# One group of silu(z) per chunk, a new layout of a chunk's pieces, and attention's first loads split over two queues

## The chip, the cores and the metric

The kernel runs on one core of one Trainium2 chip. Its time is the device time of one execution in microseconds. The kernel before takes 6737.77 us, the median of 3 runs (6736.29 to 6739.21). One execution was profiled.

## The reference, cut to what matters

Two layers with a residual each, on x of shape (4, 384, 64, 64) in fp32. Each layer first applies a group norm over 32 groups of channels. Layer 0 is a selective state-space layer over the 4096 positions of an image:

```python
xn = layernorm(tokens(gn(x))) * ln_w + ln_b
xb, z = split(xn @ in_proj_w.T)             # 768 channels each
xc = silu(causal_conv4(xb) + conv_b)
dt, Bm, Cm = split(xc @ x_proj_w.T)         # 24, 16, 16
dt = softplus(dt @ dt_w.T + dt_b)
h = exp(dt * A) * h + (dt * xc) * Bm        # a step per position; 768 channels x 16 states
y = sum_n(h * Cm) + xc * D
x = x + (y * silu(z)) @ out_proj_w.T
```

Layer 1 is an attention over a 7x7 neighbourhood with 12 heads, edge padding, a bias by relative place, softmax, a projection and a residual.

## The kernel before, in words

**Chunks and steps.** Layer 0 goes through 44 chunks: four images, each cut into pieces of 372 positions (the last has 376). A chunk holds 768 channels as six blocks `d` of 128 partitions. The 16 states come in four groups `g` of four. A step is one pair (d, g), so a chunk has 24 steps, and a step has four scans, one for each state: 96 scans in a chunk. A scan is one instruction of VectorE along the positions.

**What a step needs.** `carry` copies the state from the previous chunk into column 0 of a tile h (ScalarE). `drive` writes (dt*xc)*B into the tile, for one to four states at a time, on VectorE ("V", from the PSUM bank `dtxps`) or on GpSimd ("G", from a copy `dtx` in SBUF). `decay` computes exp(dt*A) for one state into one of three PSUM banks `das` (ScalarE). `scan` runs over it in place. `last_states` copies the last column away (ScalarE). `times_c` multiplies the tile by C (GpSimd). `sums` adds it up by transposing matmuls into the bank `yps` (TensorE). There are six h tiles (`HBUFS`). With three decay banks, ScalarE can be at most three scans ahead of VectorE: the decay for scan n needs scan n-3 to be done.

**The order.** All pieces of work are entered with a time, a tick, by `put`, sorted by tick and then emitted. A step is 16 ticks, a scan 4, a chunk (`CHUNK`) 384; a decay stands 5 ticks before its scan. The tables `AT` (the ticks of each kind of piece, relative to the first scan of the piece's chunk) and `DRIVES` (tick, step, engine, first state, number of states) fix the rest. A piece with a negative tick runs beside the chunk before. The class `Written` makes every engine keep the emitted order, SyncE's DMA queue too: an instruction that waits holds up all behind it on its engine. An engine that isn't held up may run ahead of its ticks.

**Tables of ScalarE.** Silu and softplus need table sets other than that of exp and ln, which is used everywhere else; each group (`silu`, `softplus`) ends with a load of the exp set. A chunk has two groups of silu(xc), two of silu(z) and two of softplus, each for three blocks: twelve loads. In the order, the two groups of silu(z) stand at ticks 4 and 75.

**Beside the scans** run, for the next chunk, group norm, layer norm, `in_proj` (12 products, each with a weight tile `w_in` loaded from DRAM through three buffers by `load_w`), the convolution and the small projections; for the chunk before, `gate`, `out_proj` and `residual`; and in later chunks a part of attention's keys, queries and values of images that are already done (the `key_` and `value_` pieces, with tiles xk, wk, yk, xv, vo).

**The passage to attention.** Attention goes over 32 stripes of 8 rows. A score of stripe 0 needs the keys `kt` of stripe 0 with three rows of stripe 1 copied into them by GpSimd (`surround`), the queries `q`, the bias by place, and output tiles in a pool `sb1`, whose memory is that of the state-space layer's main pool. Short-lived tiles (the set `short`) lie in a pool of their own, `prep`. `begin_attention` closes it once its last user has been emitted, and opens a pool `early` there, into which the first keys (stripes 0 and 1), the first queries, the first values `vw` and the bias are loaded through SyncE's queue. In the order before it stands at tick 597 of the last chunk, which is after that chunk's first residual. Whatever doesn't lie in `early` waits until the state-space layer's pool is free, that is until the last of its readers and writers, including the stores of the last rows of x1, has ended.

Of the kernel before, what the change touches and what calls it, by code (L numbers as in the profile page):

```python
# [8 lines left out]
F32 = mybir.dt.float32  # L9
# [5 lines left out]
P = 128  # L15
C = 384
NJ = C // P
# [5 lines left out]
NG = 4  # L23
# [7 lines left out]
TM = max(SIZES)  # L31
# [1 line left out]
STEPS = ND * NQ  # L33
STEP = 16
CHUNK = STEP * STEPS
SILU_X = SILU_Z = ((0, 1, 2), (3, 4, 5))
HBUFS = 6
CWBUFS = 3
KT = 256


AT = dict(
    load_x=(-732,),
    gn=(-656, -656, -704),
    ln_mean=(-634,),
    ln_centre=(-631,),
    ln_square=(-549, -548, -568),
    ln_var=(-540, -533, -531),
    ln_rstd=(-523,),
    ln_scale=(-520,),  # L50
    halo=(-582,),
    load_w=(-556, -419, -340, -366, -306, -365, -138, -149, -106, -103, -67, -32),
    in_proj=(-411, -388, -340, -343, -251, -321, -128, -134, -80, -33, -46, 23),
    in_bias=(-392, -387, -336, -319, -226, -286, -122, -121, -77, -30, -34, 36),
    conv=(-381, -317, -283, -227, -212, -214),
    conv_bias=(-366, -294, -257, -192, -201, -210),
    silu_x=(-253, -132),
    x_proj=(-123, -112),
    x_rows=(-100,),
    dt_mm=(-93, -56),  # L60
    softplus=(-90, -55),
    load_b=(-43, -46, -32, -29),
    load_c=(22, 15, 60, 71),
    silu_z=(4, 75),
    gate=(130, 241, 255, 327, 392, 462),
    out_proj=(462, 466, 569, 586, 588, 590),
    load_res=(371, 352, 527),
    residual=(502, 605, 617),
    out_stats=(681, 683, 692),
    dt_to_bank=(-43, 8, 91, 152, 218, 275),  # L70
    dt_times_x=(-32, 17, 91, 163, 226, 289),
    dtx_copy=(-21, 31, 101, 168, 230, 306),
    skipped=(-17, 37, 160, 180, 269, 336),
    turned_out=(97, 178, 241, 305, 363, 413),
    back=(107, 221, 250, 321, 381, 457),
    carry=(
        -4, -56, -29, 7, 36, 54, 24, 68, 102, 110, 116, 151, 176, 183, 160, 223, 247, 236,
        254, 289, 286, 297, 314, 334,
    ),
    last_states=(  # L80
        25, 33, 58, 67, 80, 100, 112, 135, 171, 168, 192, 197, 212, 236, 244, 255, 282, 289,
        309, 323, 343, 362, 384, 388,
    ),
    times_c=(
        37, 39, 72, 79, 95, 102, 115, 157, 173, 176, 203, 220, 237, 239, 257, 258, 292, 302,
        311, 339, 351, 369, 392, 394,
    ),
    sums=(
        53, 59, 76, 80, 109, 130, 149, 171, 181, 203, 224, 225, 246, 277, 278, 288, 308, 325,
        329, 353, 365, 384, 397, 412,  # L90
    ),
    x_stats=(-41, 24, 79, 381),
    x_norm=(12, 182, 194, 198, 211, 231, 247, 257, 271),
    out_norm=(319, 401, 414, 424, 442, 465, 482, 493, 507),
    value_load=(287, 147, 318),
    value_norm=(395, 214, 384),
    value_mm=(418, 238, 392),
    value_out=(424, 247, 410),
    value_store=(596, 251, 491),
    load_cv=(-473, -346, -314, -235, -259, -344),  # L100
    key_load=(44, 213),
    key_norm=(93, 69, 126, 276, 234, 288),
    key_mm=(135, 139, 181, 303, 305, 348),
    key_out=(143, 150, 191, 307, 315, 358),
    key_store=(289, 467),
)

DRIVES = (
    (-3, 0, "V", 0, 4), (0, 1, "G", 0, 3), (7, 1, "V", 3, 1), (7, 2, "V", 0, 4),
    (15, 3, "G", 0, 4), (39, 4, "G", 0, 1), (60, 5, "V", 3, 1), (61, 4, "G", 2, 2),  # L110
    (63, 4, "V", 1, 1), (67, 6, "V", 0, 4), (72, 5, "G", 0, 3), (74, 7, "V", 2, 1),
    (101, 7, "G", 0, 2), (105, 7, "G", 3, 1), (108, 8, "V", 0, 4), (126, 10, "G", 3, 1),
    (130, 9, "V", 0, 2), (132, 10, "V", 2, 1), (134, 9, "G", 2, 2), (135, 10, "G", 0, 2),
    (158, 11, "G", 0, 4), (183, 12, "V", 3, 1), (184, 12, "V", 0, 3), (184, 14, "V", 0, 4),
    (191, 13, "G", 0, 4), (228, 15, "G", 3, 1), (236, 15, "G", 0, 3), (241, 17, "V", 0, 1),
    (242, 17, "G", 1, 3), (251, 16, "V", 2, 1), (255, 16, "V", 0, 2), (255, 16, "V", 3, 1),
    (258, 18, "V", 0, 3), (264, 18, "G", 3, 1), (292, 20, "V", 0, 4), (293, 19, "G", 0, 4),
    (312, 21, "G", 0, 1), (330, 21, "V", 1, 3), (333, 22, "V", 0, 4), (344, 23, "G", 0, 4),
)
TX = 512  # L120
NXT = L // TX
# [6 lines left out]
HP = HW + 2 * PAD  # L128
# [5 lines left out]
RW, CW = RB + WS - 1, CB + WS - 1  # L134
NK = RW * CW
NCH = 2
# [32 lines left out]
def two_layers(  # L169
# [59 lines left out]
    def load(shape, src, name, pool=const):  # L229
        t = pool.tile(shape, F32, name=name)  # L230
        dq.dma_start(t, src)
        return t
# [106 lines left out]
    def load_stripe_keys(dq, kt, s):  # L339
        b, r = s // NXT, s % NXT  # L340
        for m in range(NJ):
            dq.dma_start(
                kt[:, m, PAD : PAD + RB, PAD : PAD + HW],
                kdr[b][m * P : (m + 1) * P, r * TX : (r + 1) * TX].rearrange(
                    "p (r c) -> p r c", r=RB
                ),
            )

    def load_stripe_queries(dq, q, s):
        b, r = s // NXT, s % NXT  # L350
        dq.dma_start(
            q, qdr[b][:, r * TX : (r + 1) * TX].rearrange("(k p) t -> p k t", p=P)
        )

    def load_pair_values(dq, vw, k):

        s, p = k // NPAIR, k % NPAIR
        b, r = s // NXT, s % NXT
        for e in range(2):
            for c in range(NCH):  # L360
                y, x0 = RB * r + c * RW // NCH, (2 * p + e) * CB
                dq.dma_start(vw[:KN, e, c, :], vdr[b][y : y + RW // NCH, x0 : x0 + CW, :])

    def state_space_layer(eng):
        te, ve, se, ge, _ = eng
# [4 lines left out]
        with ExitStack() as es:  # L370
# [15 lines left out]
            with tc.tile_pool(name="fold", bufs=1, side="right") as fold, tc.tile_pool(  # L386
                name="ps_fold", bufs=1, space=PSUM
            ) as fps:
                w_in = load([P, NJ, 2 * DI], in_wT.rearrange("(k p) m -> p k m", p=P), "w_in", fold)
# [70 lines left out]
            prep = preps.enter_context(  # L460
                tc.tile_pool(name="prep", bufs=1, reuse_waits="tile", side="right")
            )
            short = {"xn", "sq", "w_in", "xb", "cw", "xd", "xk", "yk", "wk", "xv", "vo"}

            free, kind_of = {}, {}

# [10 lines left out]

            def done(t):
                free[kind_of[id(t)]].append(t)

            def bank():
                return tile_of([P, 512], "mm", 3, ps_m)
# [370 lines left out]
            scans, drives, dtx, skip, turned = {}, {}, {}, {}, {}  # L853
# [280 lines left out]
            early = {}  # L1134

            def begin_attention():
                preps.close()
                home = ctx.enter_context(
                    tc.tile_pool(name="early", bufs=1, reuse_waits="tile", side="right")
                )  # L1140
                kt = early["kt"] = [
                    home.tile([P, NJ, RW, HP], F32, name=f"kt{s}") for s in range(2)
                ]
                q = home.tile([P, NJ, TX], F32, name="q0")
                vw = home.tile([P, 2, NCH, C], F32, name="vw0")
                bias = early["bias"] = home.tile([P, NH, NK], F32, name="bias")
                early["q"], early["vw"] = [q], [vw]
                for s in range(2):
                    load_stripe_keys(dq, kt[s], s)
                load_stripe_queries(dq, q, 0)  # L1150
                load_pair_values(dq, vw, 0)
                for e in range(2):
                    dq.dma_start(bias[e * QB : (e + 1) * QB].rearrange("p h k -> p (h k)"), bm)

            put(
                CHUNK * (len(chunks) - 1) + 1 + max(
                    max(AT[name]) for name in ("key_store", "value_store", "in_bias", "conv")
                ),
                begin_attention,
            )  # L1160
# [16 lines left out]
    def attention_layer(eng, gm1, qkb, pjb, early, mv):  # L1177
        te, ve, se, ge, dq = eng
        scale = HD**-0.5
        stripes = NB * NXT  # L1180
        with ExitStack() as es:
# [33 lines left out]
            def kt_of(s):  # L1215
                return ring([P, NJ, RW, HP], "kt", 4, s)

            def q_of(s):
                return ring([P, NJ, TX], "q", 3, s)
# [4 lines left out]
            def vw_of(k):  # L1224
                return ring([P, 2, NCH, C], "vw", 3, k)
# [39 lines left out]
                )  # L1265
                surround(s, m)

            def load_keys(s):
                if s > 0:
                    load_stripe_queries(dq, q_of(s), s)  # L1270
                if s > 1:
                    load_stripe_keys(dq, kt_of(s), s)

            def surround(s, m):

# [178 lines left out]
            for s in range(-3 * UNITS, N + 12):  # L1454
                stripe, k = s // UNITS, s % UNITS
# [29 lines left out]
                    load_res(stripe - 1)  # L1485
                if 0 <= stripe + 2 < stripes and has_keys(stripe + 2):
                    if k == 0:
                        load_keys(stripe + 2)
                    if k in (4, 6, 8):
                        surround(stripe + 2, (k - 4) // 2)  # L1490
                if k == 2 and 0 <= stripe + 3 < stripes and not has_keys(stripe + 3):
# [6 lines left out]
                    gn(stripe + 3, k - 6)  # L1498
                pair = (s + 1) // NJ + 1
                if (s + 1) % NJ == 0 and 0 <= pair < stripes * NPAIR:  # L1500
                    if pair > 0:
                        load_pair_values(dq, vw_of(pair), pair)

    engines = [
        Written(tc, e) for e in (nc.tensor, nc.vector, nc.scalar, nc.gpsimd, nc.sync)
# [1 line left out]
    dq = engines[-1]  # L1507
# [47 lines left out]
```

## Time and profile before

| what | us |
|---|---|
| median of 3 runs | 6737.77 |
| the profiled execution's own time | 6732.91 |
| its span, first to last instruction | 6731.2 |
| first scan starts at | 124.3 |
| last scan ends at | 5205.6 |
| first row minimum of attention (VectorE) at | 5242.75 |
| mean granted TensorE clock | 0.979 of full |

The scans take 5081.3 us for 44 chunks, 115.5 us each. A window of the profile tells each engine's busy time in a stretch; a group of the listing by line tells the mean duration of one instruction and the idle time before it; the list of waits puts each idle time down to what ended it. Every operation goes through one helper, so all have the same line, and tiles tell them apart: `da` is a decay, `h<-da,h` a scan, `h<-dtxps,BC` a drive on VectorE, `h<-dtx,BC` one on GpSimd, `h<-h,BC` a product with C, `state<-h` the copy of the last states, `sz<-sz` a silu of z.

### The profile page before, as it was taken

Reading aid. Unit: us, or ns where it says so; the run is one execution under the profiler, and the core shown is the slowest. Engines: PE = TensorE matmul, PEld = TensorE weight load, DVE = VectorE, ACT = ScalarE, POOL = GpSimd, SP = SyncE. Lnnn points to the kernel's source line nnn. Section 1 sums busy time; section 2 is a strip of 40 time slices with the busy share of each in tenths; the row PEclk is TensorE's granted clock in tenths of the full one; section 3 lists DMA queues with packets and bytes.
Section 4 is the critical chain, followed back from the end, with each engine's and each line's share of the span. In section 5 each row is a group of like instructions: output and inputs, shape, how many; then the busy total and the mean of one; then the engine's idle time right before and its main releaser. Section 6 shows DMA issues by size and latency. Waiting matters only on the chain.

```text
span 6731.2 us, 135270 instructions
## 1 busy us (share of the span) xinstructions
PE 6266.0 (93%) x47526; PEld 4311.4 (64%) x47526; DVE 5860.2 (87%) x10234; ACT 5707.5 (85%) x14235; POOL 5682.5 (84%) x2812
## 2 busy tenths in 40 slices
PE   6888888988999999999999999999996899999999
PEld 4666666666666666666666666666665555555555
DVE  3999999999999999999999999999999666555555
ACT  4888988888999999999999999999996687665556
POOL 3999999999999999999999999999999555444343
PEclk9999999999999999999999999999998999999999
DMA  5243423233444535354444444453432654323332
GB/s 185 86 129 92 134 88 129 81 122 110 147 150 130 161 118 163 120 165 128 155 139 133 151 121 151 124 161 117 157 115 68 173 156 153 103 98 104 101 102 91
DMA packets 790239, 860.10 MB, mean 128 GB/s; under 512 B 200344, under 2 KB 710072, under 8 KB 789432
## 3 DMA queue, kind: packets, MB, share of 16 engines
q1 hardware_dynamic: 789560, 851.45, 40.8%
q8 instruction: 377, 6.18, 0.4%
q14 instruction: 302, 2.47, 0.1%
HBM read 740.60 MB, written 110.81 MB: 126 GB/s over the span
## 4 chain that ended last, share of the span: by engine, by line
PE 42%; ACT 20%; DVE 20%; POOL 8%; issue 7%; DMA 3%; SPq 1%; POOLq 0%; DVEq 0%; ACTq 0%
PE mm L152 27%; DVE h L152 17%; POOL h L152 7%; PE yps L152 7%; ACT da L152 6%; PE pt L152 4%; ACT L152 3%; ACT sg L152 3%; PE ov L152 2%; DMA w_in<-wdr 2%; PE lg L152 2%; ACT dt L152 1%; ACT pT L152 1%; ACT sz L152 1%; ACT xb L152 1%
## 5 line engine op out<-in xcount | busy, mean ns | idle before, releaser
L152 DVE TENSOR_TENSOR_SCAN h<-da,h 128x373 f32<-128x373 f32 (+1 forms) x4224 | 3655.9, 914 | 119.8 <-ACT da L152 105.5
L152 POOL TENSOR_TENSOR h<-h,BC 128x1488 f32<-128x1488 f32 (+1 forms) x1056 | 3255.9, 3099 | 112.0 <-ACT state L152 104.1
L152 ACT ACTIVATE da<-dt,nega 128x372 f32<-128x372 f32 (+1 forms) x4224 | 2362.5, 569 | 211.0 <-DVE h L152 193.4
L152 POOL TENSOR_TENSOR h<-dtx,BC 128x372 f32<-128x372 f32 (+5 forms) x836 | 1757.8, 2113 | 46.6 <-ACT dtx L152 38.7
L152 PE MATMUL yps<-ident,h 128*124 128x128 f32 (+1 forms) x12672 | 1579.3, 278 | 106.5 <-POOL h L152 105.7
L152 PEld LDWEIGHTS yps<-ident,h 128*124 128x124 f32 (+1 forms) x12672 | 1446.8, 142 | 263.6 <-POOL h L152 168.5
L152 PE MATMUL mm<-xn,w_in 128*128 128x372 f32 (+3 forms) x3168 | 1133.4, 498 | 106.5 <-DMA w_in<-wdr 59.1
L152 POOL TENSOR_TENSOR sg<-sg,rs 128x784 f32<-128x784 f32 x384 | 573.4, 1493 | 627.9 <-DVE rs L152 480.5
L152 ACT ACTIVATE sg<-sg,mx 128x196 f32<-128x196 f32 x1536 | 685.3, 448 | 400.6 <-DVE mx L152 392.0
L152 DVE TENSOR_TENSOR h<-dtxps,BC 128x1488 f32<-128x1488 f32 (+5 forms) x924 | 964.5, 1059 | 2.4 <-ACT xD L152 2.4
L152 PEld LDWEIGHTS mm<-xn,w_in 128*128 128x128 f32 x3168 | 597.8, 199 | 468.4 <-issue 39.9
L152 PE MATMUL mm<-xb,cw 128*128 128x372 f32 (+1 forms) x2112 | 697.7, 476 | 4.6 <-DMA cw<-ddr 2.5
L152 ACT ACT_TABLE_LOAD x529 | 678.7, 1283 | 10.3 <-PEq L1540 0.8
L152 DVE CUSTOM_DVE_ANT_0 sg<-lg,bias 128x196 f32<-128x196 f32 x1536 | 464.4, 358 | 193.7 <-PE lg L152 178.0
L152 PE MATMUL mm<-yg,w_out 128*128 128x372 f32 (+1 forms) x1584 | 531.7, 481 | 22.5 <-DVE yg L152 22.5
L152 PEld LDWEIGHTS mm<-xb,cw 128*128 128x128 f32 x2112 | 389.8, 189 | 236.1 <-DVE h L152 2.7
L152 PE MATMUL pt<-ident,sg 128*98 128x128 f32 x3072 | 446.0, 281 | 29.1 <-ACT pT L152 21.5
L152 PEld LDWEIGHTS pt<-ident,sg 128*98 128x98 f32 x3072 | 313.9, 128 | 181.0 <-issue 80.5
L152 PEld LDWEIGHTS mm<-yg,w_out 128*128 128x128 f32 x1584 | 291.3, 191 | 185.3 <-DVE yg L152 30.9
L152 PEld LDWEIGHTS ov<-pT,vw 98*32 98x32 f32 x12288 | 189.8, 110 | 194.3 <-issue 138.3
L152 PE MATMUL mm<-xk,wk 128*128 128x256 f32 x1080 | 270.7, 393 | 46.1 <-ACT dt L152 46.1
L152 ACT ACTIVATION_READ_ACCUMULATOR sg<-sg,mx 128x1 f32 x1536 | 288.1, 188 | 0.0
(136 smaller groups left out, 7162.3 us busy)
## 6 DMA issues: line engine op xcount, KB each, us to landing
BC<-bcrows SPq DMA_DIRECT2D x320, 744.0 KB
w_in<-wdr SPq DMA_DIRECT2D x528, 192.0 KB
vw<-vdr SPq DMA_DIRECT2D x512, 147.0 KB
cw<-ddr SPq DMA_DIRECT2D x264, 256.0 KB
xs<-in_x_dram SPq DMA_DIRECT2D x210, 186.0 KB
wk<-in_qkv_wT_dram SPq DMA_DIRECT2D x180, 192.0 KB
o<-x SPq DMA_DIRECT2D x96, 256.0 KB
out_dram<-o SPq DMA_DIRECT2D x96, 256.0 KB
```

What stands on the lines that cost most here:

```text
L152: ins = made(*args, **kw)
```

## The change

First, `SILU_Z` becomes one group of six blocks, entered at tick 74. Second, nearly all ticks in `AT` and the whole of `DRIVES` are new. VectorE gets 51 of a chunk's 96 states to drive, in 18 instructions (before: 50, in 21), GpSimd 45 in 24 (before: 46 in 19). Third, the tiles xk, yk, wk, xv and vo leave the pool `prep` for the main pool, and `begin_attention` comes at tick 1 of the last chunk. It now loads only the keys of stripe 0, the queries of stripe 0 and the bias. The keys and queries of stripe 1 and the values of the first two pairs of blocks are loaded by ScalarE's DMA queue, behind its last work for the state-space layer. Last, the large tiles of the main pool are made first, in a fixed order.

```diff
-SILU_X = SILU_Z = ((0, 1, 2), (3, 4, 5))
+SILU_X = ((0, 1, 2), (3, 4, 5))
+SILU_Z = ((0, 1, 2, 3, 4, 5),)
...
-    load_w=(-556, -419, -340, -366, -306, -365, -138, -149, -106, -103, -67, -32),
-    in_proj=(-411, -388, -340, -343, -251, -321, -128, -134, -80, -33, -46, 23),
-    in_bias=(-392, -387, -336, -319, -226, -286, -122, -121, -77, -30, -34, 36),
+    load_w=(-528, -392, -350, -375, -267, -350, -128, -199, -103, -100, -58, -46),
+    in_proj=(-408, -392, -338, -363, -234, -319, -122, -128, -89, -49, -37, -9),
+    in_bias=(-398, -383, -334, -349, -230, -275, -115, -128, -83, -42, -30, 0),
...
-    silu_z=(4, 75),
+    silu_z=(74,),
...
 DRIVES = (
-    (-3, 0, "V", 0, 4), (0, 1, "G", 0, 3), (7, 1, "V", 3, 1), (7, 2, "V", 0, 4),
+    (-13, 1, "G", 3, 1), (-6, 0, "V", 0, 4), (1, 2, "V", 3, 1), (13, 1, "G", 0, 3),
...
-            short = {"xn", "sq", "w_in", "xb", "cw", "xd", "xk", "yk", "wk", "xv", "vo"}
+            short = {"xn", "sq", "w_in", "xb", "cw", "xd"}
...
+            for shape, tag, bufs in (
+                ([P, TM], "xc", 8), ([P, TM], "dt", 7), ([P, TM], "xD", 2), ([P, TM], "dtx", 2),
+                ([P, NG, TM], "BC", 8), ([P, NG, 1 + TM], "h", HBUFS),
+            ):
+                done(tile_of(shape, tag, bufs))
...
-                for s in range(2):
-                    load_stripe_keys(dq, kt[s], s)
+                load_stripe_keys(dq, kt, 0)
                 load_stripe_queries(dq, q, 0)
-                load_pair_values(dq, vw, 0)
...
-                    max(AT[name]) for name in ("key_store", "value_store", "in_bias", "conv")
+                    max(AT[name]) for name in ("in_proj", "in_bias", "conv", "x_rows", "dt_mm")
...
-            def load_keys(s):
+            def load_keys(s, dq):
                 if s > 0:
+                    load_stripe_keys(dq, kt_of(s), s)
                     load_stripe_queries(dq, q_of(s), s)
-                if s > 1:
-                    load_stripe_keys(dq, kt_of(s), s)
...
-                        load_keys(stripe + 2)
+                        load_keys(stripe + 2, se if s < 0 else dq)
...
-                    if pair > 0:
-                        load_pair_values(dq, vw_of(pair), pair)
+                    load_pair_values(se if s < 0 else dq, vw_of(pair), pair)
```

## The prediction

> **What bounds the kernel now.** I read the engines' busy time by stage first, then the waits, then timelines of the places that the change touches. The stages are: up to the first scan, the scans (split in three), the passage to attention, attention. Columns after the length: busy time and instructions of PE, its weight loads, DVE, ACT, POOL, then clock, DMA share, GB/s.
>
> ```profile
> 2430.00:3580.00 1150.00, 1103.14 (x5676) 796.33 (x5675) 1126.80 (x1401) 1090.45 (x2463) 1120.74 (x439) 0.99 0.46 142
> 5205.60:5242.75 37.15, 16.61 (x86) 10.42 (x83) 5.27 (x11) 0.54 (x2) 9.23 (x18) 0.80 0.60 133
> ```
>
> Among the scans VectorE is busy 98%, GpSimd 97%, TensorE 96%, ScalarE 95%. So VectorE and GpSimd bound this stage nearly equally. With a chunk of 115.6 us (chunks 1 to 42), VectorE works 112.8 and GpSimd 112.7; what can be won is some 2.8 us of idle time in each. In the passage no engine works much: 37 us of latency. Attention (1488 us) is untouched but for its first loads.
>
> ```profile
> DVE h L152 <- ACT da L152: 105.5, 191, 3.4
> POOL h L152 <- ACT state L152: 104.1, 143, 2.7
> ...
> ACT xb L152 <- PE mm L152: 62.8, 55, 5.1
> ...
> PE mm L152 <- DMA w_in<-wdr: 59.1, 34, 4.2
> ```
>
> Columns: total us, times, longest. Nearly all of VectorE's idle time (105.5 over 44 chunks, 2.4 each) is a scan whose decay is late; GpSimd's is a late copy of the last states. Both are ScalarE's work. ScalarE isn't short of time on average but late in places. Laying VectorE's timeline of chunks 1 to 42 on top of each other, its 2.8 us per chunk fall so: 0.31 at ticks 8 to 16 (behind the first silu of z), 0.30 at 32 to 40 (copies piled up behind it), 0.65 at 48, 0.22 at 72 (second silu of z), 0.65 at 296 (first softplus), 0.27 at 312, the rest scattered. The 0.65 at 48 has a root elsewhere: TensorE waits for a `w_in` tile, `xb` waits for TensorE, the decays wait behind `xb`.
>
> **Silu of z in one group.** One group looks so:
>
> ```profile
> 2916.45 0.56 ACT L152 ACTIVATE da<-dt,nega 128x372 f32<-128x372 f32 x1
> 2917.02 1.28 ACT L152 ACT_TABLE_LOAD   x1
> 2918.32 1.32 ACT L152 ACTIVATE sz<-sz 128x372 f32<-128x372 f32 x3
> 2919.65 1.28 ACT L152 ACT_TABLE_LOAD   x1
> 2920.95 1.07 ACT L152 ACTIVATE da<-dt,nega 128x372 f32<-128x372 f32 x2
> ```
>
> From the end of one decay to the start of the next it takes 3.9 us. Two loads go per chunk, 2 x 1.29 = 2.6 us start to start, 44 x 2.6 = 113 us of ScalarE's time. The Trainium skill's page "ScalarE: Activation LUTs", section "What ACT_TABLE_LOAD costs", puts a drain of 1.38 us on top of 1.283, 2.66 us for a switch; by it the change would free 44 x 5.3 = 234 us. Here the silu starts 0.02 us after the load, so I take 113. Either way this isn't on the path as such: ScalarE already waits for scans 193 us in all. What counts is how long a block keeps decays back, against the work that VectorE still has.
>
> I sum it for each block from start-to-start times in the trace: scan 0.825, decay 0.51, silu 0.42, softplus 0.47, load 1.295; drives on VectorE of 1, 2, 3, 4 states 0.44, 0.84, 1.21, 1.60. Cover is VectorE's work from the end of scan n-4 to the start of scan n; need is what ScalarE does meanwhile when it is fully ahead: decay n-1 and all up to the end of decay n. Before: first silu of z, cover 6.99, need 5.13; second 5.39 and 5.05; first softplus 5.39 and 5.19. The traced stalls (0.31, 0.22, 0.65) exceed what these give, because ScalarE comes in less than fully ahead. After, in the built order: silu of z 6.27 against 6.89 (state copy 0.09, load, six silus 2.52, load, one `xk` 0.49, decays), short by **0.62**; the silus of xc 7.00 and 6.16 against 5.05; softplus 5.83 and 5.72 against 5.28. So the long block itself costs VectorE about as much as the two short ones: I take 0.7 against 0.31 + 0.22. The pile behind the first group (0.30) goes.
>
> **The new ticks.** `w_in` of product 2: before, its load stands with its product at tick 44 and its buffer is freed by product 11 (tick 23), so SyncE issues it some 15 ticks (4.5 us) ahead, behind a 744 KB load. After, product 11 comes at -9 and the load at 34 uses a buffer free by then; SyncE's queue isn't held by other waits from tick 1 on. That takes away TensorE's wait (59.1 us) and with it the 0.65 at tick 48. For every other `w_in` after, I find at least 40 ticks between a possible issue and the product. The B and C loads keep 40 ticks or more. The softplus blocks have 0.55 and 0.44 to spare; I take 0.4 of stall for the 0.65. Elsewhere ScalarE's work in each run of scans is below VectorE's; I leave 0.65 for all the rest, with the scattered stalls of now (0.96 with tick 312) partly going with ScalarE's lighter load. Idle time per chunk: 0.7 + 0.4 + 0.65 = 1.75 in place of 2.82, a gain of 1.07.
>
> **Drives.** VectorE before: 9 x 0.44 + 2 x 0.84 + 3 x 1.21 + 7 x 1.60 = 20.4 us per chunk; after: 5, 1, 4 and 8 of them, 20.7. That costs 0.23 per chunk, all on the path. GpSimd's (0.94, 1.73, 2.52, 3.31 for 1 to 4) stay at 39.1. Net: 0.84 x 44 = **37 us** gained. ScalarE's earlier `in_proj` 11 adds no instruction; before the first scan it may add one bias, 0.5 us, hidden behind loads.
>
> **The passage.** SyncE's queue and GpSimd's timeline:
>
> ```profile
> 5218.90 5.92 SPq L152 DMA_DIRECT2D kt<-kdr  x6
> 5224.86 1.14 SPq L152 DMA_DIRECT2D q<-qdr  x1
> 5226.05 3.13 SPq L152 DMA_DIRECT2D vw<-vdr  x4
> 5229.28 1.14 SPq L152 DMA_DIRECT2D bias<-bm  x2
> 5230.52 1.38 SPq L152 DMA_DIRECT2D x<-xs  x2
> ...
> 5242.52 2.41 POOL L152 COPY kt<-kt 128x210 f32<-128x210 f32 x9 [15.48 <-DMA x<-xs]
> ```
>
> The loads sit behind the first store of x1, which waits for the first residual. The last two stores (their data ready at 5225.6 at the latest) are issued only at 5230.5, behind 4.1 MB, and land at 5242.2; then the pool is free and attention starts within 1 us. After, keys 0, queries 0 and bias come 100 us earlier, and the stores go out at once. The pool is then free when VectorE's last statistics end, 5228.3: **14 us earlier**. But what is late next is new. Keys 1, whose rows stripe 0 needs, aren't early now; they are issued by ScalarE at 5228.3. And ScalarE has 12 DMAs ahead of its first exp. At SyncE's durations their issue is 3 x 0.99 + 1.14 + 8 x 0.78 = 10.4 us, so no exp before 5239. Most of them also wait for an earlier DMA to land, the last one in the built order for the second load of pair 2's values on SyncE's queue; by then 4.8 MB of keys, queries, values and projection weights have moved. At the 280 KB/us that moved just after 5242 that is 17 us: first exp at 5246, against 5243.1 now. The skill's page "DMA: Bandwidth & Descriptors", section "Issuing engines are not separate DMA queues", speaks against this part: a second issuing engine saves the issue time alone, the data share the same 16 engines. By the row of issue times the split gains 4 us; by the rule, with bytes as the limit, it loses 3. I take the loss, **+3 us**, with ends of -5 and +10. Later steps of attention find their values loaded, worth nothing that I can see.
>
> **The sum.** Profiled: 6732.9 - 37 + 3 = 6699. The median of the runs lies 4.9 above the profiled execution: 6704.
>
> **Rivals.** A: as summed; its own range, with 0.3 to 1.5 us per chunk and the passage's ends, is 6667 to 6730. B: a lighter ScalarE lets both VectorE and GpSimd go to 0.8 us of idle time; the chunk is then 113.0 + 0.8 = 113.8, and the time 6737.8 - 1.8 x 44 + 3 = 6662. For it: both wait for ScalarE almost alone. Against it: the long block's 0.6 is certain. C: nothing is gained, since GpSimd's wait for last states stays. For it: the new order has six steps with two ticks or less between `last_states` and `times_c`, the present one three, and GpSimd has as little slack as VectorE; the drives' 10 us on VectorE then lie beside GpSimd's work: 6737.8 + 3 = 6741. Against it: the copies that are late now stand behind the piles on ScalarE that go. D, slower: the long block. If ScalarE comes to it two scans short of full lead (1.65 us), the stall is 2.3 us per chunk. With the two short blocks and the `w_in` stall gone the idle time is 2.82 - 0.53 - 0.65 + 2.3 = 3.9; with the drives +1.35 x 44 + 3 gives 6800. It decides from a stall of 0.95 us (0.53 + 0.65 - 0.23). Against it: in the six scans before the block, ScalarE has 4.6 us of work, VectorE 8.3, so it should be fully ahead. That the change doesn't do what it says is excluded by the built order: 441 table loads for 529.
>
> **Chances.** A 0.58, B 0.16, C 0.15, D 0.11. The range reaches from B to just past C: 6652 to 6748. What a measurement can tell from no change is about 0.2%, 13.5 us. Faster than 6724: nearly all of A and all of B, 0.76 with what C's edge adds; within: 0.13; slower than 6751: D, 0.11.
>
> **What would show it.** The table loads fall to 441. TensorE's wait for `w_in` falls below 15 us. VectorE's wait for decays falls from 105.5 to some 60 to 70, with a stall of about 0.7 us at tick 76 in every chunk; two or more there means D. GpSimd's wait for `state` unchanged near 104 means C. A chunk of 114.7 us means A. In the passage the last store of x1 lands near 5228 and the first exp comes 40 us after the last scan; 35 would show that the bytes don't limit. I'm wrong if VectorE's idle time per chunk is outside 1.1 to 2.6 us.

## The result, and the profile after

The changed kernel takes 6690.1 us (median) against 6737.77: ratio 0.9929, 95% interval 0.9916 to 0.9943. It is faster, and the forecast was 6704. One of its six executions took 7913 us at a granted clock of 0.75 and is left out of the ratio; the others lie between 6687.9 and 6694.3 at 0.982 to 0.985. The profiled execution took 6691.2, its span 6689.4.

| stretch | before | after | difference |
|---|---|---|---|
| start to first scan | 124.3 | 120.8 | -3.5 |
| scans, 44 chunks | 5081.3 | 5037.8 | -43.5 |
| of these chunks 1 to 42, each | 115.58 | 114.37 | -1.20 |
| of these the last chunk | 111.0 | 118.6 | +7.6 |
| last scan to first exp of attention | 37.6 | 44.4 | +6.9 |
| the rest | 1488.1 | 1486.4 | -1.7 |

The differences add to -41.8, that of the spans. The scans bring the gain, and two places give some of it back: the last chunk and the passage.

The windows view of the changed kernel, for the same stretch of scans as before and for the passage; columns as in the prediction.

```profile
2430.00:3580.00 1150.00, 1105.42 (x5719) 792.83 (x5718) 1127.40 (x1381) 1074.51 (x2459) 1125.37 (x491) 1.00 0.46 144
5158.61:5203.03 44.42, 19.59 (x107) 12.75 (x107) 6.05 (x18) 0.54 (x2) 12.09 (x26) 0.77 0.49 132
```

ScalarE is busy 16 us less in 1150, though more of the work now fits into it. VectorE and GpSimd are busy 98%, as VectorE was before. The list of waits of the changed kernel (total us, times, longest):

```profile
DVE h L154 <- ACT da L154: 74.5, 64, 5.7
...
POOL h L154 <- ACT state L154: 65.2, 78, 7.2
...
PE mm L154 <- DMA w_in<-wdr: 40.5, 30, 7.0
...
ACT xb L154 <- PE mm L154: 25.5, 22, 5.0
```

Waits for decays (105.5 before) fell by 29%, those for last states (104.1) by 37%. There are far fewer waits for decays (64 for 191), but they are longer. The wait for `w_in` fell only from 59.1 to 40.5, and its longest rose from 4.2 to 7.0 us.

### The profile page after: what moved, and what is told of

Read it like the earlier page. It is cut to its first block, busy times and chain, and to the rows that moved or that the text cites. A ratio compares the mean times of both kernels' runs of the same rounds, so it can differ in the third digit from the quotient of the medians.

```text
span 6689.4 us, 134599 instructions
## 1 busy us (share of the span) xinstructions
PE 6224.9 (93%) x47526; PEld 4275.4 (64%) x47526; DVE 5838.8 (87%) x10102; ACT 5612.8 (84%) x14147; POOL 5676.5 (85%) x3032
## 4 chain that ended last, share of the span: by engine, by line
DVE 33%; PE 29%; ACT 26%; issue 6%; POOL 4%; DMA 1%; SPq 1%; POOLq 0%; DVEq 0%; ACTq 0%
DVE h L154 29%; PE mm L154 17%; ACT da L154 9%; PE pt L154 4%; POOL h L154 4%; PE yps L154 4%; ACT L154 3%; ACT sg L154 3%; PE ov L154 2%; PE lg L154 2%; ACT dt L154 2%; ACT sz L154 2%; DVE xn L154 1%; ACT xD L154 1%; ACT pT L154 1%
## 5 line engine op out<-in xcount | busy, mean ns | idle before, releaser
L154 DVE TENSOR_TENSOR_SCAN h<-da,h 128x373 f32<-128x373 f32 (+1 forms) x4224 | 3616.6, 913 | 88.4 <-ACT da L154 74.5
L154 POOL TENSOR_TENSOR h<-h,BC 128x1488 f32<-128x1488 f32 (+1 forms) x1056 | 3257.7, 3102 | 68.4 <-ACT state L154 65.2
L154 POOL TENSOR_TENSOR h<-dtx,BC 128x372 f32<-128x372 f32 (+6 forms) x1056 | 1754.6, 1682 | 52.8 <-ACT dtx L154 35.8
L154 PE MATMUL yps<-ident,h 128*124 128x128 f32 (+1 forms) x12672 | 1603.7, 279 | 138.7 <-POOL h L154 136.7
L154 PE MATMUL mm<-xn,w_in 128*128 128x372 f32 (+3 forms) x3168 | 1099.0, 487 | 84.0 <-DMA w_in<-wdr 40.5
L154 DVE TENSOR_TENSOR h<-dtxps,BC 128x1488 f32<-128x1488 f32 (+6 forms) x792 | 967.6, 1235 | 2.1 <-ACT dtx L154 1.4
L154 PEld LDWEIGHTS mm<-xn,w_in 128*128 128x128 f32 x3168 | 576.6, 192 | 417.6 <-DVE h L154 56.6
L154 ACT ACT_TABLE_LOAD x441 | 565.8, 1283 | 8.7 <-PEq L1542 0.8
L154 PE MATMUL mm<-xp,w_qkv 128*128 128x512 f32 x612 | 279.5, 593 | 0.0
```

What stands on the lines that cost most here:

```text
L154: ins = made(*args, **kw)
```

## The experiments

Each kernel was timed beside the kernel before on one chip, so ratios to it are what is compared; 0.001 is 6.7 us. The intervals reach up to 0.0015 to either side.

| kernel | us | ratio [95% interval] | idle us per chunk, VectorE / GpSimd | last scan to first exp |
|---|---|---|---|---|
| before | 6737.77 | 1 | 2.82 / 2.93 | 37.6 |
| changed | 6690.1 | 0.9929 [0.9916, 0.9943] | 2.12 / 1.89 | 44.4 |
| e1: one group, old ticks | 6775.05 | 1.0051 [1.0038, 1.0064] | 3.93 / 3.61 | 38.0 |
| e2: new ticks, groups at 4 and 74 | 6748.69 | 1.0017 [1.001, 1.0023] | 3.50 / 3.29 | 43.3 |
| e2c: new ticks, groups at -6 and 74 | 6742.16 | 1.0007 [0.9998, 1.0015] | 3.16 / 3.07 | 44.4 |
| e3: first loads through SyncE | 6677.61 | 0.9907 [0.9893, 0.992] | 2.03 / 1.75 | 29.6 |
| e4: `xk` norm later | 6681.91 | 0.9922 [0.991, 0.9935] | 1.81 / 1.71 | 42.9 |
| e5: one `w_in` load earlier | 6666.72 | 0.9899 [0.9886, 0.9913] | 1.59 / 1.36 | 43.2 |
| e6: e3, e4, e5 together | 6652.21 | 0.9878 [0.9863, 0.9893] | 1.40 / 1.29 | 29.6 |
| e7: early loads later | 6680.92 | 0.9922 [0.9909, 0.9936] | 2.10 / 1.89 | 44.3 |
| e8: e6 and e7 together | 6637.18 | 0.986 [0.9846, 0.9873] | 1.30 / 1.21 | 29.6 |

Idle times are means over chunks 1 to 42, summed from each engine's timeline. The granted clock doesn't explain the differences: it is 0.979 in the profile of before, 0.983 in that of the changed kernel and 0.984 in that of e2c, which is no faster than before. The moved pools and the fixed order of the large tiles were not tried alone; instructions of one kind take the same time before and after (GpSimd's products with C 74.4 and 74.5 us per chunk).

### The group without the ticks (e1), the ticks without the group (e2, e2c)

e1, against the kernel before:

```diff
-SILU_X = SILU_Z = ((0, 1, 2), (3, 4, 5))
+SILU_X = ((0, 1, 2), (3, 4, 5))
+SILU_Z = ((0, 1, 2, 3, 4, 5),)
...
-    silu_z=(4, 75),
+    silu_z=(75,),
```

> The kernel before with one edit: all six silus of z in one group at tick 75, every other piece where it was. Cover theory (a block on ScalarE costs VectorE what it exceeds VectorE's work in hand): the block is short by 0.9 us in chunks with statistics (cover 5.39, need 6.31) and by 1.4 in the others, where the stalls at ticks 8 to 16, 32 to 40 and 72 (0.83 us in all) go: some 0.3 us per chunk worse, about 6750 us; between 6735 and 6760. Rival (table loads count: 2.6 us per chunk less work on ScalarE frees VectorE and GpSimd): 6700 us or less.

It was 34 us *slower* than before by the ratio: the theory's sign, but outside its range, which ended at 6760. 88 table loads fewer, and the time rises, so the rival is out. Its waits:

```profile
DVE h L153 <- ACT da L153: 160.0, 147, 4.3
...
ACT xb L153 <- PE mm L153: 97.5, 55, 5.5
...
PE mm L153 <- DMA w_in<-wdr: 69.5, 34, 3.8
```

VectorE now idles 1.39 us per chunk at the block, as the theory had it (0.9 to 1.4). But it also idles 1.42 at tick 48, where there were 0.65. The stalls at ticks 8 to 40 are all but gone (0.1 left), which the theory counted as a gain; more than their time came back at tick 48. TensorE's wait for the late `w_in` grew from 59.1 to 69.5 us, and that of `xb` for TensorE behind it from 62.8 to 97.5. Why it grew was not tried, so e1's 34 us aren't the block's cost alone.

e2, against the changed kernel (e2c has -6 in place of 4):

```diff
-SILU_Z = ((0, 1, 2, 3, 4, 5),)
+SILU_Z = ((0, 1, 2), (3, 4, 5))
...
-    silu_z=(74,),
+    silu_z=(4, 74),
```

> The changed kernel with silu of z in two groups again, at ticks 4 and 74. Twelve table loads per chunk. Cover theory: the second group fits (need 5.63, cover 6.27 or 5.39), the first at tick 4 falls among scans without other VectorE work (need 5.13, cover 3.35) and stalls VectorE by 1.8 us per chunk: 0.8 us for the long block go, 1.8 come, so 44 us slower than the changed kernel, about 6734. Rival (table loads count, 1.3 us each on ScalarE wherever they stand): slower by some 0.3 to 0.5 us per chunk, 6705 to 6712.

> The changed kernel with silu of z in two groups at ticks -6 and 74. Twelve table loads per chunk, but the first group stands where VectorE has a four-state drive to do (need 5.15, cover 4.96 with statistics, 4.52 without), the second fits. Cover theory: 0.2 to 0.7 us of stall in place of 0.8, so 10 to 25 us faster than the changed kernel, 6665 to 6680, although ScalarE does 113 us more. Rival (table loads count): slower than the changed kernel, 6705 or more.

e2 lost the whole gain: by the ratios it is 59 us slower than the changed kernel, more than the 44 expected and far more than the rival's 15 to 22. At tick 8 VectorE idles 2.14 us per chunk; at 72 it is down to 0.12. The two groups are alike, three silus each; what differs is the lead, the time from the end of the last decay before the group to the start of its scan. On average over chunks 1 to 42 it is 1.5 us at the first group and 4.2 at the second.

For e2c my count of cover promised 6665 to 6680, and that was wrong. The rival's words, 6705 or more, fit its 6742; but the rival's reason, loads that cost the same wherever they stand, fits neither e1 nor the two groups of e2. ScalarE's timeline of e2c, then VectorE's (start, duration, engine, operation, out<-in, and in brackets the idle time before it):

```profile
2418.60 0.59 ACT L154 ACTIVATE da<-dt,nega 128x372 f32<-128x372 f32 x1
2419.21 1.28 ACT L154 ACT_TABLE_LOAD   x1
2420.50 1.32 ACT L154 ACTIVATE sz<-sz 128x372 f32<-128x372 f32 x3
2421.82 1.28 ACT L154 ACT_TABLE_LOAD   x1
2423.12 0.61 ACT L154 ACTIVATE xD<-xc,dsk 128x372 f32<-128x372 f32 x1
2423.63 0.56 ACT L154 ACTIVATE da<-dt,nega 128x372 f32<-128x372 f32 x1
```

```profile
2421.37 0.92 DVE L154 TENSOR_TENSOR_SCAN h<-da,h 128x373 f32<-128x373 f32 x1
2424.22 0.94 DVE L154 TENSOR_TENSOR_SCAN h<-da,h 128x373 f32<-128x373 f32 x1 [1.93 <-ACT da L154]
```

The last decay before the block ends at 2419.19 and its scan starts at 2421.37, so ScalarE leads by 2.2 us, and with that scan VectorE has 3.0 us of work. The next decay ends at 2424.19, 5.0 us on, with an `xD` in between: short by 2.0. In the changed kernel, whose rows the next part shows, the lead at the block is 3.9 us (its decay ends at 2424.88; its scan, the second in the row at 2427.97, starts at 2428.8). Cover counted from a full lead holds only where ScalarE has just *waited* for VectorE. Between 2410.8 and this block it never waits.

So neither part is worth anything alone: +34 and, with the passage's loss, +5 to +11 by the ratios; together -48. The group clears ticks 0 to 20, which the new layout fills; the layout gives the long block at 74 a place where ScalarE is ahead: in e1 it comes to the block with a mean lead of 2.8 us, in the changed kernel with 4.4, and there it has waited for a scan just before the block in every chunk from 1 to 42, in e1 in 13 of them.

### The long block's stall (e4)

The changed kernel's ScalarE and VectorE around one block:

```profile
2424.31 0.57 ACT L154 ACTIVATE da<-dt,nega 128x372 f32<-128x372 f32 x1 [0.25 <-DVE h L154]
2424.82 0.18 ACT L154 COPY state<-h 128x4 f32<-128x4 f32 x1
2425.02 1.28 ACT L154 ACT_TABLE_LOAD   x1
2426.32 2.53 ACT L154 ACTIVATE sz<-sz 128x372 f32<-128x372 f32 x6
2428.86 1.28 ACT L154 ACT_TABLE_LOAD   x1
2430.16 0.60 ACT L154 ACTIVATE xk<-xk,gm 128x256 f32<-128x256 f32 x1
2430.67 0.55 ACT L154 ACTIVATE da<-dt,nega 128x372 f32<-128x372 f32 x1
```

```profile
2427.97 1.75 DVE L154 TENSOR_TENSOR_SCAN h<-da,h 128x373 f32<-128x373 f32 x2
2431.25 2.58 DVE L154 TENSOR_TENSOR_SCAN h<-da,h 128x373 f32<-128x373 f32 x3 [1.53 <-ACT da L154]
```

The bracket on the first decay (it waited 0.25 us for a scan) shows full lead. Still VectorE stalls 1.53 us. In most chunks the stall is 0.16 where there is no `xk` norm, 0.65 where there is one, and 1.53 where there is one and no group norm statistics run on VectorE beside it. e4 moves the norm:

```diff
-    key_norm=(116, 74, 126, 261, 239, 281),
+    key_norm=(116, 86, 126, 261, 239, 281),
```

> The changed kernel with one edit: the second piece of key_norm (the xk norm on ScalarE) comes at tick 86 and not at 74, so that it no longer stands right behind the six silus of z and ahead of the next decay. Theory (cover of the long block): ScalarE's need there falls by one xk norm, from 6.89 to 6.4 us, against a cover of 6.27 in chunks with two x statistics and 5.39 in the others; the stall at ticks 72 to 76, 0.78 us per chunk in the changed kernel and 1.53 in chunks with keys and without statistics, falls by about 0.5 in the 30 chunks that have a norm there: 15 us, 6690 becomes about 6675. Rival (GpSimd limits just as closely): the stall goes but GpSimd's wait for the states takes its place, 6687 to 6692.

The same stall in e4, on VectorE:

```profile
2427.85 0.94 DVE L154 TENSOR_TENSOR_SCAN h<-da,h 128x373 f32<-128x373 f32 x1 [1.05 <-ACT da L154]
```

The stall of 1.53 fell to 1.05 and that of 0.65 to 0.16, as counted, in 27 chunks. But 0.14 came back at tick 88, where the norm now stands ahead of another decay. The stretch of scans became 7.5 us shorter, half of what was expected; by the times it is 5 us, less than their interval. VectorE's idle time did fall by 13 us in all (0.31 per chunk), but its busy time rose by 0.12 per chunk: it waits 3.9 times in place of 3.2, and the last part tells what a wait costs. GpSimd's waiting fell too, so the rival is out.

### The late weights (e5)

SyncE's queue in the changed kernel (start, time that the issues took), then TensorE:

```profile
3049.42 0.80 SPq L154 DMA_DIRECT2D x<-xs  x2
3050.27 0.51 SPq L154 DMA_DIRECT2D w_in<-wdr  x1
3050.84 9.69 SPq L154 DMA_DIRECT2D vdr<-vo  x15
3060.57 0.41 SPq L154 DMA_DIRECT2D w_in<-wdr  x1
```

```profile
3063.25 4.06 PE L154 MATMUL mm<-xn,w_in 128*128 128x372 f32 x6 [7.03 <-DMA w_in<-wdr]
```

The second `w_in` is issued 9.7 us late: ahead of it stand 15 stores of values, at 0.65 us of issue each. TensorE waits 7.03 us for it, and VectorE some 5 in the end. So it goes in the three chunks (14, 25, 36) where an image's first values are stored; TensorE's waits of 6.5 and 6.6 us in the other two the profile puts down to VectorE, though the second `w_in` is issued as late there, so the 40.5 us hold only one of the three. In other chunks the stores of x1 alone, which wait for the residual, cost TensorE 0.8 to 1.0. The edit:

```diff
-    load_w=(-528, -392, -350, -375, -267, -350, -128, -199, -103, -100, -58, -46),
+    load_w=(-528, -392, -350, -375, -267, -350, -160, -199, -103, -100, -58, -46),
```

> The changed kernel with one edit: the load of w_in for product 6 of in_proj comes at tick -160 and not at -128, so that in SyncE's queue it stands ahead of the stores of x1, which wait for the residual, and of the value stores. Theory (the load is late because of what stands ahead of it in its queue): TensorE's wait for w_in falls from 40.5 to 10 to 15 us, the 5 us stalls of VectorE in chunks 14, 25 and 36 and the 0.8 to 1.0 us waits of TensorE in some 20 other chunks go; 15 to 25 us faster than the changed kernel, about 6670. Rival: the stall moves to the next load behind the same stores (product 7, or the carried-over x loads), and the time stays at 6685 to 6692.

All of it came: the ratio falls by 0.0030 (20 us), the scans by 23.8 us, and chunks 14, 25 and 36 from 120.2, 121.4 and 119.7 to 113.5, 113.5 and 114.1. The waits of e5:

```profile
DVE h L154 <- ACT da L154: 54.0, 62, 2.7
...
POOL h L154 <- ACT state L154: 42.3, 74, 1.8
...
PE mm L154 <- DMA w_in<-wdr: 14.8, 12, 2.0
```

One load, 32 ticks earlier, also shortens GpSimd's wait: a late product delays ScalarE's `sz` bias, and everything queued behind that on ScalarE.

### The passage (e3)

ScalarE in the changed kernel; the first three rows are DMAs that it issues:

```profile
5182.39 3.25 ACTq L154 DMA_DIRECT2D kt<-kdr  x3
5185.66 2.42 ACTq L154 DMA_DIRECT2D q<-qdr  x1
5188.20 14.78 ACTq L154 DMA_DIRECT2D vw<-vdr  x8
5203.03 0.46 ACT L154 ACTIVATE sg<-sg,mx 128x196 f32<-128x196 f32 x1 [36.17 <-DMA vw<-vdr]
```

```profile
5190.23 0.36 DVE L154 CUSTOM_DVE_ANT_0 sg<-lg,bias 128x196 f32<-128x196 f32 x1 [8.07 <-DMA kt<-kdr]
```

VectorE's first row minimum, the last row, starts at 5190.23. The exp behind it comes 12.8 us later, because ScalarE is still issuing loads of values that nobody needs yet. e3 lets SyncE issue them:

```diff
-                        load_keys(stripe + 2, se if s < 0 else dq)
+                        load_keys(stripe + 2, dq)
...
-                    load_pair_values(se if s < 0 else dq, vw_of(pair), pair)
+                    load_pair_values(dq, vw_of(pair), pair)
```

> The changed kernel with attention's remaining first loads issued by SyncE's queue instead of ScalarE's. Theory (ScalarE is held by its own DMA issues, the last of which wait for others to land): the first exp no longer waits for them; it comes when keys 1 have landed and VectorE has the first minimum, some 33 us after the last scan in place of 44.4, so about 11 us faster than the changed kernel, 6679. Rival (the bytes limit, whoever issues): the first exp stays at 42 to 45 us after the last scan, 6688 to 6692.

SyncE's queue in e3, ScalarE's first exp, and the window of the passage:

```profile
5177.16 2.00 SPq L154 DMA_DIRECT2D kt<-kdr  x3
5179.20 0.94 SPq L154 DMA_DIRECT2D q<-qdr  x1
5180.19 0.49 SPq L154 DMA_DIRECT2D w_pj<-in_proj_wT_dram  x1
5180.72 7.21 SPq L154 DMA_DIRECT2D vw<-vdr  x8
```

```profile
5182.92 0.46 ACT L154 ACTIVATE sg<-sg,mx 128x196 f32<-128x196 f32 x1 [21.26 <-DVE mx L154]
```

```profile
5153.37:5182.92 29.55, 17.47 (x91) 11.25 (x91) 5.24 (x13) 0.54 (x2) 11.26 (x25) 0.90 0.26 64
```

The first exp now waits for a row minimum and comes 29.6 us after the last scan: 14.9 earlier than in the changed kernel, 8 earlier than before. The ratio falls by 0.0022, 15 us. In e3 the transfers move 64 GB/s in the passage, against 132 there in the changed kernel: attention starts while the values are still to come, so their bytes held nothing up.

### The last chunk (e7)

Why does the last chunk take 118.6 us, and the one before it 111.4? SyncE's queue, GpSimd and VectorE of the changed kernel:

```profile
5037.97 2.20 SPq L154 DMA_DIRECT2D kt<-kdr  x3
5040.21 0.96 SPq L154 DMA_DIRECT2D q<-qdr  x1
5041.22 1.16 SPq L154 DMA_DIRECT2D bias<-bm  x2
5042.48 4.95 SPq L154 DMA_DIRECT2D BC<-bcrows  x4
```

```profile
5055.16 3.49 POOL L154 TENSOR_TENSOR h<-dtx,BC 128x752 f32<-128x752 f32 x2 [8.07 <-DMA BC<-bcrows]
```

```profile
5058.68 4.28 DVE L154 TENSOR_TENSOR_SCAN h<-da,h 128x377 f32<-128x377 f32 x5 [5.23 <-POOL h L154]
...
5068.11 0.55 DVE L154 TENSOR_TENSOR yg<-mm,sz 128x372 f32<-128x372 f32 x1 [4.72 <-PE mm L154]
```

Attention's early loads stand right ahead of the chunk's last B and C. GpSimd waits for those, and VectorE for GpSimd. e7 puts `begin_attention` behind the last of them:

```diff
-                CHUNK * (len(chunks) - 1) + 1 + max(
+                CHUNK * (len(chunks) - 1) + 100 + max(
```

> The changed kernel with one edit: begin_attention (keys of stripe 0, queries of stripe 0 and bias through SyncE's queue) comes at tick 100 of the last chunk and not at tick 1. Theory (a cost that the prediction left out): at tick 1 these six transfers stand ahead of the last chunk's four loads of B and C, so GpSimd waits 8.1 us for BC and VectorE 5.2 and 4.7 us behind it, and the last chunk takes 118.6 us against 111.4 for the chunk before it; at tick 100 no B or C load is left behind them: last chunk near 111.5, 7 us faster than the changed kernel, about 6683. The passage stays at 44 us. Rival: the loads of B and C are late for another reason (their rows are stored late), and the last chunk stays at 117 to 119.

The last chunk takes 110.7 us, and no wait of GpSimd over 0.3 us is left in it. By the times that is 5 us, inside their interval; the trace shows 7.9 at the very place.

### Together (e6, e8)

> The changed kernel with three edits at once: attention's first loads by SyncE's queue, the xk norm at tick 86, the w_in load of product 6 at tick -160. Theory: the three act at different places (passage, tick 76, tick 256 of the chunk before), so the gains add: 6690 - 12 - 15 - 20 = 6643, 6635 to 6655. Rival: the two in the chunk uncover the same next limit, GpSimd's wait for the states, and add up to half: 6658 to 6672.

> The four edits at once: attention's first loads by SyncE's queue, the xk norm at tick 86, the w_in load of product 6 at tick -160, begin_attention at tick 100 of the last chunk. Theory: the last edit acts in the last chunk alone and its 7 us add to the three's: 0.9878 of the kernel before becomes about 0.9868, 6648 where that takes 6737.8. Rival: the early loads, now 30 us later, collide with the stores and loads of the passage and the first exp comes over 31 us after the last scan; then the gain is under 4 us.

e6 is 0.0051 below the changed kernel, where e3, e4 and e5 alone sum to 0.0059: the gains nearly add. e8 is another 0.0018 below e6, and its first exp comes 29.6 us after the last scan, so nothing collides. e8 is the fastest: 6637 us, 1.4% under the kernel before, twice the gain of the change itself. Its VectorE still idles 1.30 us per chunk, GpSimd 1.21.

## Why the prediction was right, and where it was not

The sum of 6699 for the profiled execution stands against 6691.2, and rival A came. The mechanism, fewer late decays, was right, but it gives only 0.70 of the 1.20 us that a chunk lost. The other 0.51 is busy time of VectorE, which the sum had with the opposite sign. Against the sum, in the profiled execution, idle time gave 16 us less and busy time 31 us more; the last chunk took 8 and the passage 4; the start and the rest of attention gave 5. That these errors come to only 8 us is luck.

- **Table loads** went to 441, and the two that a chunk loses free 2.6 us of ScalarE's time, as the row said: all loads together take 565.8 us in place of 678.7, 113 less. Nothing shows the drain that the Trainium skill's page adds; the silu starts 0.02 us after the load here too.
- **The block, 0.7 us**: 0.78 on average. But it isn't "about 0.7 in every chunk": it is 0 to 1.54 us. The cover of 6.27 was taken from a chunk in which VectorE has two statistics (0.88 us), and the need from one with an `xk` norm. The mean came out by balance. Where chunks are of the kind that I mixed (statistics and norm), the forecast of 0.62 meets 0.65.
- **The pile at ticks 8 to 40** went: 0.03 us are left.
- **"For every other `w_in` after, I find at least 40 ticks"** failed. Product 6 has 23 between the last residual, which frees the queue (623 - 384 = 239 in the next chunk), and the product (384 - 122 = 262), and I let issues take no time: 15 of them take 9.7 us. The wait that was to fall below 15 us stayed at 40.5; e5 brings it to 14.8, and VectorE's idle time from 2.12 to 1.59. That is why the idle time is 2.12 and not 1.75, and VectorE's wait for decays 74.5 and not 60 to 70.
- **Softplus 0.4**: 0.43 at ticks 288 to 335 once e5 has taken the weights' part away. **The rest, 0.65**: about 0.38.
- **Drives, +0.23**: VectorE's busy time per chunk *fell*, from 112.76 to 112.25. The drives' durations add to 22.24 us before and 22.23 after; the rise counted by starts is no more than lost overlap between three instructions fewer. What I left out has the other sign: VectorE waits 3.2 times a chunk in place of 9.0. e1, with the old drives, shows it alone: 5.9 waits, busy 112.43. By the cost of a wait in the last part (0.10 us), 5.8 waits fewer less the overlaps of three instructions fewer (0.08 each) make 0.34 of the 0.51; the rest is not explained.
- **The passage, +3**: +6.9. The pool came free as forecast: GpSimd's `surround` starts 23.8 us after the last scan, against 36.9 before (13 us earlier, forecast 14). The step after it failed: "with bytes as the limit". By my own test, 35 us would show that bytes don't limit; e3 has 29.6. The row of issue times was the better guide, but I took SyncE's 10.4 us for ScalarE's twelve DMAs, and they took 20.6 with the waits between them. The Trainium skill's page "DMA: Bandwidth & Descriptors", section "Issuing engines are not separate DMA queues", says that a second issuer saves the issue time alone. The passage moved 133 GB/s before and 132 with two issuers, at 0.60 and 0.49 of the DMA engines' time, so no run here tests the page's limit; and the issue time wasn't saved but lost, because ScalarE had work of its own behind its issues.
- **The early loads** were counted as a gain alone. What they stand ahead of in SyncE's queue was left out: +7.6 us in the last chunk (e7).
- **The first scan**, 3.5 us earlier, was not in the sum. Its cause was not tried.

GpSimd's wait for `state` fell from 104.1 to 65.2, so C is out. D needed 0.95 us of stall at the block; the mean is 0.78. But where the layout is missing, in e1, D's case comes about: ScalarE's lead at the block is 1.5 us shorter and the stall 1.39, though not D's 2.3. B's idle time of 0.8 isn't reached even by e8.

## What to carry to other kernels

Count the lead of an in-order engine at the place, not from its maximum: where the engine has just been waiting for its consumer, a long block costs only what exceeds the work in the consumer's hand; where it hasn't, the missing lead comes on top. A load moved to an earlier place in a queue pushes back what it now precedes, and an issue that waits holds its engine's own work: list, for every queue, what stands behind the moved transfers and when that is needed. And check a term in chunks of every kind, since a mean may be right for the wrong reason.

## What the runs showed of the hardware

A wait costs VectorE more than its idle time. Where nothing holds it, an instruction's row starts 0.08 us before the row ahead of it ends (10.5 us over 131 such pairs in a chunk of the kernel before); a waiting instruction loses that overlap, and a scan that has waited has a longer row, 0.934 us on average against 0.911. Together that is 0.10 us for a wait. e1 fits: 3.2 waits fewer at 0.10 make 0.33 us per chunk, and the busy time fell from 112.76 to 112.43. So fewer, longer waits are cheaper than many short ones of the same sum. The Trainium skill's page "Perfetto Trace Analysis", section "Optimizing Scalar/DVE Operations", tells of such an overlap with the next instruction; its figures put it, as an estimate, at 60 ns for operands in SBUF and 125 in PSUM. The trace's 0.08 lies between, and scans and drives read one of each. DMA issues aren't free either: 0.65 us for a store of values, 0.9 for a load of `vw` on SyncE, and on ScalarE eight loads took 14.8 us with the waits among them, in which no ACTIVATE ran.
